# Two layers with attention, routed experts and coupling: the choice of tokens moved ahead, and the last output taken through diagonals of the gate

## The chip, the cores and the metric

The kernel runs on one core of a Trainium2 chip. The metric is the device time of one execution, in microseconds (us). Of before, three runs are given; the profile is of a fourth execution.

## The reference

The input x has 8 batches of 512 tokens with 256 channels, float32. Two layers follow one another; in each, `mod = silu(c) @ wmod` gives for every batch two shifts, two scales and two gates (the gates kept away from zero), and

```
h = layernorm(x) * (1 + ca) + sa;   x = x + ga * attention(h)
h = layernorm(x) * (1 + cb) + sb;   x = x + gb * ffn(h)
```

Layer 0: attention is causal softmax attention with 16 query heads of 16 channels, rotary embedding and one key and value head. Its ffn is a layer of 16 experts where each expert chooses tokens:

```
probs = softmax(h @ Wg + bg, over the tokens)
vals, idx = top_k(probs per expert, 64)          # per batch and expert
tok = h[idx]
out = (relu(relu(tok@w1+b1)@w2+b2)@w3+b3) * vals
outputs = zeros.at[idx].add(out)
```

Layer 1: attention is linear attention (elu + 1, causal running sums). Its ffn is three rounds of a coupling: a four layer network with gelu gives one gate per token, and

```
coupling = 0.1 + adaptive_range * (0.7*gf + 0.3*tf - 0.5) * 2
out = out + coupling * twist(out)                # twist swaps the channel halves, with signs
```

## The kernel before, in words

**Engines and their order.** The program order of all five engines' queues is written by hand: each engine carries out its instructions in the order in which the code issues them. Independent parts are Python generators ("lanes") that `Steps.run` advances in turn. A lane has a rank, which says who is served first, and a pace: `steps.rank(rank, every, phase)` lets it advance at every second (or `every`-th) step only. `steps.until("maxima", 7)` holds a lane until another has reported that event. A `yield` more or less in a lane therefore moves every instruction behind it relative to the other lanes.

**Layer 0, attention.** `batch(b)` is one lane per batch: `made_ready` (layer norm, projections, rotary embedding), `maxima` (the scores once, for the row maxima: PE L691/L701, DVE reductions L727 and L734, maxima L740, transposes L748, and L753, which puts the maxima into the queries), `heads_of` (the scores again, PE L793; ACT exponentials L815; POOL masks L820; PE values L775) and `finished` (PE transposes L845, DVE L850 and L852 which divide by the sums, L860, output projection L874, x += on DVE L880, a copy of x to memory, `xs`, L884, layer norm L563 to L572 with `bn_rstd` on POOL, gate logits L900, the modulation of the normalised tokens L914 on POOL, and the tokens to memory, `xg`, L916). At the end of `heads_of`, POOL adds the gated output bias to x (L830). Two batches overlap: heads of one beside maxima of the next. The modulation reads a row that a DMA brings (L891).

**Layer 0, experts.** `experts_side` (L940) waits for `ready` of batch 7 (the last), opens its buffers, waits for `maxima` of batch 7, and calls `choose(0)` for batches 0 to 3 (`choose(1)` is for batches 4 to 7). `choose` (L1002) holds 64 rows, an expert of a batch each, with 512 probabilities: softmax, then eight rounds of DVE's MAX8 (L1027), FIND_INDEX8 (L1028) and MATCH_REPLACE8 (L1031), two copies (`twice`, L1033/L1034), PE transposes (L1038), and small operations that make the indices `gidx` and `slot` and the values `valc`. `begin` gathers the tokens of three items and starts the weights of two. An item is one expert with the 128 tokens that two pairs of batches chose for it, twice (two indirect DMAs of 128 rows); there are 32 items, 16 for each half of the batches: experts 0 to 15 of the first half, then 8 to 15 and 0 to 7 of the second, so that eight weight sets are used again (`KEPT`). `run` (L1119) does per item: weights (`fetch_up_to`, on SP's queue, twice an item), gather of item i+3 (two indirect DMAs on POOL, L1103), ACT's scaling of item i-2 by its values (L1195), first layer (PE L1159, relu on DVE L1166), transposes of item i+1 (PE L1148, ACT L1152), scatter of item i-2 (two indirect DMAs on POOL that add into `xs`, L1202), last layer of item i-1 (PE L1179, DVE L1184), second layer of item i (PE L1159, relu on ACT L1168). In the middle (item 19) the first half of x is read back from `xs`. `choose(1)` is a generator that `run` advances twice an item; when a gather needs indices that are not made yet, the loop in `gather` drains the rest of it at once. Tokens have 4 buffers, `y` 3, `y0` 2.

**Layer 1.** Linear attention by batches (L1324 to L1568), its norm's `bn_rstd` on POOL (L1336 to L1340), `xh` on ACT (L1344), products (L1358, L1451, L1466). Then rounds of the coupling for pairs of batches n = 0 to 3 (`rounds`, L1795), where only PE's order is by hand. One round of a pair holds its state transposed, g (channels by tokens): `first_layer` (PE L1753; it also makes `still`, the part of the new g that does not depend on the gate), `later_layers` (L1805: w2 L1811, w3 L1821, w4 L1827, tanh on ACT L1831, m = (tanh + slope) x other half on DVE L1838, new g = still + or - m on DVE L1844). `finish` (L1851) multiplies g by the gate gb on ACT (`gated`, L1858), transposes it on PE (L1869), adds x on DVE into `res` (L1874, two buffers) and sends it out. The last pair's third round and its `finish` stand alone at the end of the program.

The change touches `heads_of`, `finished`, `experts_side`, `choose`, `open_first`, `begin`, `run` and `rounds`.

Of the kernel before, what the change touches and what calls it, by code (L numbers as in the profile page):

```python
# [13 lines left out]
F32 = mybir.dt.float32  # L14
# [8 lines left out]
P = 128  # L23
# [424 lines left out]
def layer0(net, steps):  # L448
# [311 lines left out]
    def heads_of(b, kT, qT):  # L760
# [66 lines left out]
        yield  # L827
        yield from values(3)
        for i in range(NT):
            nc.gpsimd.tensor_tensor(net.x[b][:, i, :], net.x[b][:, i, :], bg, ALU.add)  # L830
        yield
        return oT, wg

    def finished(b, oT, wg):
# [72 lines left out]
        for j in range(NT):  # L907
            nc.sync.dma_start(
                out=net.logits[b // NBP][b2 * NE : (b2 + 1) * NE, j * P : (j + 1) * P],
                in_=lg[32 * j : 32 * j + NE, :],  # L910
            )
        for row, how in zip(mod_rows, (ALU.mult, ALU.add)):
            for i in range(NT):
                nc.gpsimd.tensor_tensor(xh2[:, i, :], xh2[:, i, :], row, how)  # L914
            yield
# [24 lines left out]
    def experts_side():  # L940


        yield from steps.until("ready", B - 1)
        ready.close()
        experts.open_first()
        yield from steps.until("maxima", B - 1)
        yield from experts.choose(0)
        yield from experts.begin()
        yield from steps.until("heads", B - 1)
        early.close()  # L950
        experts.open()
        yield from experts.run(choices)
        experts.close()
        past.add(("experts",))
# [14 lines left out]
class Experts:  # L969
# [32 lines left out]
    def choose(self, half):  # L1002
# [31 lines left out]
        nc.vector.tensor_copy(twice[:, 1], vals.unsqueeze(1).to_broadcast([R, 2, TOPK]))  # L1034
        yield
        ps = net.mm()
# [30 lines left out]
        self.valc.append(valc)  # L1067
        yield

# [5 lines left out]
    def open_first(self):  # L1075

        self.tp = self.pool("t", 4)
        self.first_wp = self.pool("v", 2)

    def open(self):  # L1080
# [27 lines left out]
    def begin(self):  # L1108
        last = list(range(NE - self.KEPT, NE))
        self.items = [(0, e) for e in range(NE)] + [(1, e) for e in last]  # L1110
        self.items += [(1, e) for e in range(NE - self.KEPT)]
        self.tok, self.w = {}, {}
        for i in range(3):
            self.gather(i)
            if i < 2:
                self.w[i] = self.weights(i)
            yield

    def run(self, choices):  # L1119
# [15 lines left out]
        def gather(i):  # L1135
            if i < n_items:
                while len(self.gidx) <= items[i][0]:
                    next(choices)
                self.gather(i)
# [90 lines left out]
        for i in range(n_items + 2):  # L1230
            fetch_up_to(i + self.KEPT - 1)
            gather(i + 3)
            weighted(i - 2)
# [10 lines left out]
            if i == NE + 3:  # L1244
                read_back(0)
            fetch_up_to(i + self.KEPT - 1)
            self.steps.past.add(("item", i))
# [336 lines left out]
class Coupling:  # L1584
# [202 lines left out]
    def rest(self, out):  # L1787
        net, nc, tc = self.net, self.net.nc, self.net.tc
        with ExitStack() as ctx:
            self.ctx = ctx  # L1790
            gp = self.new_pool("f1g", 4, "right")
            pool = self.new_pool("f1", 2, "left")
            self.rounds(gp, pool, out)

    def rounds(self, gp, pool, out):  # L1795
# [9 lines left out]
        def later_layers(n, h1):  # L1805
# [43 lines left out]
            yield  # L1849

        def finish(n):  # L1851
            g, _ = self.state[n]
# [47 lines left out]
        with tc.manual_schedule(engines={nc.tensor.engine}):  # L1900
            done = (0, self.now)
            seen = {0: 1}
            between.append(prepare(2))
            for n in order[1:]:
                seen[n] = seen.get(n, 0) + 1
# [20 lines left out]
                done = (n, now)  # L1926
            later = later_layers(*done)
            for _ in range(3):
                take(later)
                fill(2)  # L1930
            fill(20)
            all_of(finish(done[0]))

# [78 lines left out]
```

## Time and profile before

| | |
|---|---|
| three runs | 1163.57, 1161.17, 1160.54 us, median 1161.17 |
| profiled execution | 1161.49 us; span of its instructions 1159.8; mean granted clock of TensorE 0.973 |
| busy: PE, DVE, ACT, POOL | 1084.9, 735.9, 573.3, 531.5 us (94, 63, 49, 46% of the span) |
| experts, 484 to 718 us: PE, DVE, ACT, POOL | 208.6, 81.8, 75.7, 178.2 busy of 234 |
| rounds of the coupling, 985 to 1145: the same | 159.8, 102.1, 85.7, 1.2 busy of 160 |
| last 15 us, 1145 to 1160: the same | 4.5, 8.3, 3.7, 0 busy; granted clock 0.58 |

Times in the profile are us from the span's start. A line of a timeline holds start, duration, engine, line of the code, operation, tiles (output <- inputs), how many instructions it groups, and in brackets the idle time before it and what ended it. A line of waits holds who waited for what, us in total, times, and the longest. A line of windows holds the stretch, its length, then busy time and instructions of PE, PEld, DVE, ACT and POOL, the granted clock, the DMA share and GB/s. Line numbers are those of before, unless it is said that they are of after; after's are higher by 1 to 6 in the attention and the experts (L830 is L831, L914 is L917, L1038 is L1045).

### The profile page before, as it was taken

The page shows a single profiled execution, that of the slowest core. Times are in us where ns is not written, and L with a number is a line of the kernel's source. Part 1 is how long each engine was busy: PE and PEld are TensorE (multiplying, and loading weights), DVE is VectorE, ACT ScalarE, POOL GpSimd, SP SyncE. Part 2 cuts the span into 40 slices and gives each one's busy share as a digit, 9 for nine tenths or more (in the row PEclk, how much of TensorE's full clock was granted, in tenths as well). Part 3 has the DMA queues.
Part 4 walks back from the last instruction along what each step waited for, and adds up shares of the span by engine and source line. Part 5 has one row for each costly group of instructions (what it writes and reads, how often), then busy time and mean ns, then how long its engine had stood idle before and what let it go on. Part 6 is the DMA issues. An engine that isn't in the chain of part 4 may idle for free. (4 is left out here: it accounts for less than half of the span.)

```text
span 1159.8 us, 20967 instructions
## 1 busy us (share of the span) xinstructions
PE 1084.9 (94%) x8282; PEld 675.1 (58%) x8282; DVE 735.9 (63%) x1444; ACT 573.3 (49%) x1061; POOL 531.5 (46%) x625
## 2 busy tenths in 40 slices
PE   4889999999999999889898989799999999999996
PEld 3545555555555555478676777466776666444433
DVE  3887777777777777622652322767768666766665
ACT  2255666666665657625232243544545543555544
POOL 4413344435353626568777787556545554000000
PEclk9889999999999999989899999899999999999997
DMA  6200010101101011387857944400000000000102
GB/s 208 90 1 1 1 28 25 29 26 29 42 12 50 5 50 44 91 272 208 204 89 186 241 83 61 114 6 6 6 2 6 7 6 2 0 1 19 54 1 73
DMA packets 67970, 69.02 MB, mean 60 GB/s; under 512 B 10216, under 2 KB 64544, under 8 KB 67872
## 3 DMA queue, kind: packets, MB, share of 16 engines
q1 hardware_dynamic: 55024, 49.32, 13.7%
q0 software_dynamic: 12288, 16.79, 8.4%
q8 instruction: 65, 1.06, 0.4%
q10 hardware_dynamic: 560, 1.58, 0.4%
q14 instruction: 33, 0.27, 0.1%
HBM read 46.38 MB, written 21.01 MB: 58 GB/s over the span
## 5 line engine op out<-in xcount | busy, mean ns | idle before, releaser
L815 ACT ACTIVATE e<-mm 128x512 f32<-128x512 f32 x320 | 171.6, 599 | 104.3 <-PE mm L793 90.7
L734 DVE TENSOR_REDUCE pm<-mm 128x4 f32<-128x512 f32 x256 | 162.2, 681 | 50.0 <-PE mm L701 49.0
L691 PE MATMUL mm<-kT,qT 32*128 32x128 f32 (+3 forms) x1024 | 192.3, 471 | 0.6 <-DVE pm L727 0.4
L793 PE MATMUL mm<-qT,kT 32*128 32x128 f32 (+3 forms) x1024 | 177.1, 465 | 0.0
L820 POOL TENSOR_SCALAR_AFFINE_SELECT e<-e 128x512 f32<-128x512 f32 x128 | 86.1, 693 | 186.7 <-ACT e L815 170.2
L1202 POOL DMA_INDIRECT xs<-y,slot x64 | 102.7, 1604 | 35.2 <-issue 11.3
L793 PEld LDWEIGHTS mm<-qT,kT 32*128 32x128 f32 x1024 | 81.5, 184 | 44.7 <-issue 21.0
L691 PEld LDWEIGHTS mm<-kT,qT 32*128 32x128 f32 x1024 | 92.7, 187 | 19.8 <-issue 4.7
L1753 PE MATMUL mm<-g,cn_w 128*128 128x512 f32 x192 | 93.2, 606 | 0.0
L775 PE MATMUL mm<-e,vaug 128*32 128x512 f32 (+3 forms) x1024 | 79.1, 437 | 2.2 <-POOL e L820 2.2
L1103 POOL DMA_INDIRECT tok<-xg,gidx x64 | 63.9, 998 | 19.4 <-issue 14.3
L1534 POOL TENSOR_SCALAR_AFFINE_SELECT am<-am 128x1024 f32<-128x1024 f32 x32 | 45.9, 1435 | 58.1 <-ACT am L1532 58.1
L1166 DVE TENSOR_SCALAR hid<-mm,eb 128x512 f32<-128x512 f32 x32 | 24.0, 750 | 73.0 <-PE mm L1159 73.0
L1168 ACT ACTIVATE hid<-mm,eb 128x512 f32<-128x512 f32 x32 | 22.0, 687 | 91.9 <-PE mm L1159 91.9
L1179 PE MATMUL mm<-ew,hid 128*128 128x256 f32 x256 | 63.9, 395 | 1.1 <-ACT hid L1168 1.1
L1184 DVE SCALAR_TENSOR_TENSOR y<-mm,eb,gb 128x512 f32<-128x512 f32 x32 | 24.0, 750 | 63.5 <-PE mm L1179 63.4
L1159 PE MATMUL mm<-hid,ew 128*128 128x256 f32 x256 | 62.2, 387 | 0.0
L1159 PE MATMUL mm<-tokT,ew 128*128 128x256 f32 x256 | 61.2, 382 | 0.1
L1358 PE MATMUL mm<-hT,w1qkv 128*128 128x512 f32 x128 | 60.9, 618 | 0.0
L1838 DVE SCALAR_TENSOR_TENSOR m<-th,slope,g 128x512 f32<-128x512 f32 x48 | 34.0, 748 | 40.4 <-ACT th L1831 40.4
L701 PEld LDWEIGHTS <-identb 128*128 128x128 bf16 x320 | 18.8, 98 | 64.4 <-issue 57.1
L1753 PEld LDWEIGHTS mm<-g,cn_w 128*128 128x128 f32 x192 | 33.1, 190 | 39.8 <-issue 37.1
(243 smaller groups left out, 2234.2 us busy)
## 6 DMA issues: line engine op xcount, KB each, us to landing
ew<-in_L_ffn_w SPq DMA_DIRECT2D x72, 256.0 KB, 6.8
x<-in_L_attn_x SPq DMA_DIRECT2D x8, 512.0 KB, 7.6
xs<-x SPq DMA_DIRECT2D x8, 512.0 KB, 3.0
xg<-xh SPq DMA_DIRECT2D x8, 512.0 KB, 3.3
x<-xs SPq DMA_DIRECT2D x8, 512.0 KB, 9.2
out<-res SPq DMA_DIRECT2D x16, 256.0 KB, 2.2
ga_row<-gate_a SPq DMA_DIRECT2D x16, 128.0 KB, 3.1
mod_row<-rows SPq DMA_DIRECT2D x16, 128.0 KB, 4.3
```

The lines of the kernel that those rows point to most:

```text
L691: nc.tensor.matmul(strips[j][:, at : at + nk], qT[g][rows_of(j), p, i * P : (i + 1) * P], kT[rows_of(j), p, :nk], start=(n == 0), stop=Fal ...
L734: nc.vector.tensor_reduce(pm[:, j, g, p, first : first + 4], strips[j].rearrange("q (a k) -> q a k", k=P), AX.X, ALU.max,)
L775: nc.tensor.matmul(av[32 * j : 32 * j + 32, c * P :], va[:, c, :], e[:, j, at : at + T - c * P], start=(a == 0), stop=(a == 3), skip_group ...
L793: nc.tensor.matmul(strips[j][:, at : at + T - c * P], kT[rows_of(j), p, c * P : (c + 1) * P], qT[g][rows_of(j), p, c * P :], start=(n == 0 ...
L815: nc.scalar.activation(e[:, j, :], strips[j], AF.Exp, scale=scale)
L820: nc.gpsimd.affine_select(out=own, in_=own, compare_op=ALU.is_ge, fill=0.0, base=0, pattern=[[0, 4], [1, P]], channel_multiplier=-1,)
L1103: self.net.nc.gpsimd.indirect_dma_start(out=tok[:, n, :], out_offset=None, in_=self.net.xg[half], in_offset=bass.IndirectOffsetOnAxis(ap=s ...
L1159: nc.tensor.matmul(ps[:, o * C : (o + 1) * C], w[i][n][:, k, o * P : (o + 1) * P], src[:, k, :], start=(k == 0), stop=(k == 1),)
L1179: nc.tensor.matmul(ps[:, n * C : (n + 1) * C], hid2[i][:, k, n * P : (n + 1) * P], w[i][2][:, k, :], start=(k == 0), stop=(k == 1),)
L1202: nc.gpsimd.indirect_dma_start(out=net.xs[2 * half + n], in_=y[i][:, n, :], in_offset=None, out_offset=bass.IndirectOffsetOnAxis(ap=self.s ...
L1358: nc.tensor.matmul(ps, w[:, k, n * P : (n + 1) * P], hT[:, k, :], start=(k == 0), stop=(k == 1))
L1753: nc.tensor.matmul(ps, self.w1[:, k, o * P : (o + 1) * P], g[k][bb], start=(k == 0), stop=(k == 1),)
```

## The change

1. The adds of the output bias for batch 7 (L830) and the modulation of batches 6 and 7 (L914) go from POOL to DVE.
2. `choose(0)` no longer waits for the maxima of batch 7: it begins two steps after batch 7 is ready, one step in three. Three yields instead of one stand ahead of `choose(1)`'s transposes, and both lose the last yield.
3. Tokens have 5 buffers, four items are gathered ahead instead of three, and the first two weight sets are started when the buffers are opened.
4. The second call of `fetch_up_to` in an item is made from item 6 on only.
5. For the last pair of batches, six POOL operations make diagonal matrices of the gate (`gate_diagonals`), issued at the start of the rounds. In its last round (`last_layers`) PE multiplies `still` and m by these diagonals and accumulates both in one bank (16 products for each, with the token side as the stationary matrix); that is g times the gate, transposed. DVE adds x to it into four buffers of their own. The new g, `gated` and the transposes of `finish` fall away for this pair.

The diff, with the copied w2, w3 and w4 layers of `last_layers` cut:

```diff
--- before.py
+++ after.py
@@ -826,8 +826,9 @@
         wg, bg = net.gated_by(pool, wo, bo, ga)
         yield
         yield from values(3)
+        engine = nc.vector if b == B - 1 else nc.gpsimd
         for i in range(NT):
-            nc.gpsimd.tensor_tensor(net.x[b][:, i, :], net.x[b][:, i, :], bg, ALU.add)
+            engine.tensor_tensor(net.x[b][:, i, :], net.x[b][:, i, :], bg, ALU.add)
         yield
         return oT, wg
 
@@ -909,9 +910,11 @@
                 out=net.logits[b // NBP][b2 * NE : (b2 + 1) * NE, j * P : (j + 1) * P],
                 in_=lg[32 * j : 32 * j + NE, :],
             )
+        engine = nc.vector if b >= B - 2 else nc.gpsimd
         for row, how in zip(mod_rows, (ALU.mult, ALU.add)):
             for i in range(NT):
-                nc.gpsimd.tensor_tensor(xh2[:, i, :], xh2[:, i, :], row, how)
+                engine.tensor_tensor(xh2[:, i, :], xh2[:, i, :], row, how)
             yield
         nc.sync.dma_start(
             out=net.xg[b // NBP][b2 * T : (b2 + 1) * T, :].rearrange("(i p) c -> p i c", p=P),
@@ -943,8 +946,11 @@
         yield from steps.until("ready", B - 1)
         ready.close()
         experts.open_first()
-        yield from steps.until("maxima", B - 1)
+        steps.rank(4, 3)
+        yield
+        yield
         yield from experts.choose(0)
+        steps.rank(4)
         yield from experts.begin()
         yield from steps.until("heads", B - 1)
         early.close()
@@ -1032,7 +1038,8 @@
         twice = pool.tile([R, 2, 2, TOPK], F32, name="twice")
         nc.vector.tensor_copy(twice[:, 0], idx.unsqueeze(1).to_broadcast([R, 2, TOPK]))
         nc.vector.tensor_copy(twice[:, 1], vals.unsqueeze(1).to_broadcast([R, 2, TOPK]))
-        yield
+        for _ in range(1 + 2 * half):
+            yield
         ps = net.mm()
         for a in range(2):
             nc.tensor.transpose(
@@ -1065,7 +1072,6 @@
         self.slot.append(slot)
         self.gidx.append(gidx)
         self.valc.append(valc)
-        yield
 
     def pool(self, name, bufs):
         return self.stack.enter_context(
@@ -1074,8 +1080,9 @@
 
     def open_first(self):
 
-        self.tp = self.pool("t", 4)
+        self.tp = self.pool("t", 5)
         self.first_wp = self.pool("v", 2)
+        self.w = {i: self.weights(i) for i in range(2)}
 
     def open(self):
         self.hp, self.yp = self.pool("h", 2), self.pool("y", 3)
@@ -1109,11 +1116,9 @@
         last = list(range(NE - self.KEPT, NE))
         self.items = [(0, e) for e in range(NE)] + [(1, e) for e in last]
         self.items += [(1, e) for e in range(NE - self.KEPT)]
-        self.tok, self.w = {}, {}
-        for i in range(3):
+        self.tok = {}
+        for i in range(4):
             self.gather(i)
-            if i < 2:
-                self.w[i] = self.weights(i)
             yield
 
     def run(self, choices):
@@ -1135,7 +1140,7 @@
         def gather(i):
             if i < n_items:
                 while len(self.gidx) <= items[i][0]:
-                    next(choices)
+                    next(choices, None)
                 self.gather(i)
 
         def turn(i):
@@ -1229,7 +1234,7 @@
         yield
         for i in range(n_items + 2):
             fetch_up_to(i + self.KEPT - 1)
-            gather(i + 3)
+            gather(i + 4)
             weighted(i - 2)
             if i < n_items:
                 hid[i] = layer(i, 0, tokT[i], "hid")
@@ -1243,7 +1248,8 @@
                 hid2[i] = layer(i, 1, hid[i], "hid2")
             if i == NE + 3:
                 read_back(0)
-            fetch_up_to(i + self.KEPT - 1)
+            if i >= 6:
+                fetch_up_to(i + self.KEPT - 1)
             self.steps.past.add(("item", i))
             next(choices, None)
             yield
@@ -1790,6 +1796,7 @@
             self.ctx = ctx
             gp = self.new_pool("f1g", 4, "right")
             pool = self.new_pool("f1", 2, "left")
+            self.last = self.new_pool("f1l", 1, "left")
             self.rounds(gp, pool, out)
 
     def rounds(self, gp, pool, out):
@@ -1846,6 +1853,91 @@
                         ALU.add if h == 0 else ALU.subtract,
                     )
             self.state[n] = (new, offs)
+            yield
+        def gate_diagonals(n):
+            sides = {}
+            for bb in range(2):
+                b = 2 * n + bb
+                for h in range(2):
+                    kept = self.last.tile([P, P], F32, name=f"kept{h}{bb}")
+                    nc.gpsimd.tensor_scalar(
+                        kept, net.ident, net.modT[1][:, GB, h, b : b + 1], 1.0, ALU.mult, ALU.mult
+                    )
+                    moved = kept
+                    if h:
+                        moved = self.last.tile([P, P], F32, name=f"moved{bb}")
+                        nc.gpsimd.tensor_scalar(moved, kept, -1.0, 1.0, ALU.mult, ALU.mult)
+                    sides[bb, h] = kept, moved
+            return sides
+        def last_layers(n, h1, sides):
+            g, _ = self.state[n]
...
+            ms = {}
+            for bb in range(2):
+                th = pool.tile([P, T], F32, name=f"th{bb}")
+                nc.scalar.activation(th, ps[bb], AF.Tanh, bias=self.b4, scale=0.5)
+                for h in range(2):
+                    ms[bb, h] = pool.tile([P, T], F32, name=f"m{h}{bb}")
+                    nc.vector.scalar_tensor_tensor(
+                        ms[bb, h], th, self.slope, g[1 - h][bb], ALU.mult, ALU.mult
+                    )
+            banks = {}
+            for part in range(2):
+                for bb in range(2):
+                    b = 2 * n + bb
+                    for ip in range(NT // 2):
+                        if part == 0:
+                            banks[bb, ip] = net.mm()
+                        ps = banks[bb, ip]
+                        for ii in range(2):
+                            i = 2 * ip + ii
+                            for h in range(2):
+                                src = ms[bb, h] if part else h1["still"][h][bb]
+                                nc.tensor.matmul(
+                                    ps[:, ii * C + h * P : ii * C + (h + 1) * P],
+                                    src[:, i * P : (i + 1) * P], sides[bb, h][part],
+                                    start=(part == 0 and ii == 0 and h == 0), stop=(part == 1),
+                                    skip_group_check=True,
+                                )
+                        if part == 0:
+                            continue
+                        res = self.last.tile([P, 2, C], F32, name="last", bufs=4)
+                        nc.vector.tensor_tensor(
+                            res, net.x[b][:, 2 * ip : 2 * ip + 2, :],
+                            ps.rearrange("p (i c) -> p i c", i=2), ALU.add,
+                        )
+                        at = ip * 2 * P
+                        nc.sync.dma_start(
+                            out=out[b, at : at + 2 * P, :].rearrange("(i p) c -> p i c", p=P),
+                            in_=res,
+                        )
             yield
 
         def finish(n):
@@ -1901,6 +1993,7 @@
             done = (0, self.now)
             seen = {0: 1}
             between.append(prepare(2))
+            sides = gate_diagonals(NBP - 1)
             for n in order[1:]:
                 seen[n] = seen.get(n, 0) + 1
                 while self.state.get(n, (None, None))[1] is None:
@@ -1924,12 +2017,12 @@
                 if seen[done[0]] == CYCLES:
                     between.insert(0, finish(done[0]))
                 done = (n, now)
-            later = later_layers(*done)
-            for _ in range(3):
-                take(later)
-                fill(2)
+            later = last_layers(*done, sides)
+            take(later)
+            fill(2)
+            take(later)
             fill(20)
-            all_of(finish(done[0]))
+            take(later)
 
 
 @with_exitstack
```

## The prediction

> **What bounds the kernel now.** I read the busy shares and the 40 slices first, then the stretches between stages, then the waits of the expert stage (484 to 734 us), then single instructions of POOL, PE and DVE. PE is busy 94% of the span; it is nearly full everywhere but in three places, and the change touches each. First, the expert stage. Its waits in this stretch (columns: waiter, what it waited for, sum us, times, longest):
>
> ```profile
> PE mm L1148 <- DMA tok<-xg,gidx: 24.0, 23, 5.0
> POOL tok L1103 <- issue: 14.3, 48, 0.5
> POOL xs L1202 <- DMA xs<-y,slot: 9.0, 8, 2.8
> ```
>
> PE waits for gathered tokens. Behind that stands POOL, whose steady item has no gap but some 0.30 an instruction (start, duration, line, idle before):
>
> ```profile
> 584.78 1.63 POOL L1202 DMA_INDIRECT xs<-y,slot  x1 [0.30 <-ACT hid L1168]
> 586.71 1.58 POOL L1202 DMA_INDIRECT xs<-y,slot  x1 [0.30 <-issue]
> 588.59 1.01 POOL L1103 DMA_INDIRECT tok<-xg,gidx  x1 [0.30 <-PE mm L1179]
> 589.91 0.99 POOL L1103 DMA_INDIRECT tok<-xg,gidx  x1 [0.31 <-issue]
> ```
>
> So an item costs POOL 3.81 for its scatters and 2.61 for its gathers, 6.42 together (first layers of items 10 to 30 stand 6.71 apart). PE needs three layers of 1.73 and .43 of transposes, 5.62 (items 2 to 4: 511.50, 517.12, 522.74). POOL sets the pace, and it also begins late:
>
> ```profile
> 484.74 1.25 POOL L1103 DMA_INDIRECT tok<-xg,gidx  x1 [0.19 <-issue]
> 486.30 0.95 POOL L1103 DMA_INDIRECT tok<-xg,gidx  x1 [0.30 <-issue]
> 487.27 2.77 POOL L914 TENSOR_TENSOR xh<-xh,mod_row 128x256 f32<-128x256 f32 x4
> 490.01 2.77 POOL L830 TENSOR_TENSOR x<-x,bo_g 128x256 f32<-128x256 f32 x4
> 492.94 0.99 POOL L1103 DMA_INDIRECT tok<-xg,gidx  x1 [0.16 <-issue]
> ```
>
> Item 1's gather waits behind 5.5 us of attention arithmetic; item 1 starts at 501.72, 11.5 after item 0. Second, DVE in the attention before (busy after the five names' times; third pair is DVE):
>
> ```profile
> 415.00:420.00 5.00, 5.00 (x59) 2.04 (x55) 1.68 (x3) 2.38 (x6) 0.64 (x1) 1.00 0.00 0
> 435.00:440.00 5.00, 5.00 (x44) 1.97 (x48) 4.68 (x8) 3.63 (x9) 2.84 (x7) 1.00 0.00 0
> 440.00:445.00 5.00, 5.00 (x72) 3.28 (x68) 2.08 (x4) 4.55 (x10) 0.64 (x1) 1.00 0.00 0
> ```
>
> The choice of tokens goes into these gaps now. Third, the tail: w4's last matmuls end at 1144.77, the span at 1159.8.
>
> ```profile
> 1149.01 2.37 PE L1869 MATMUL mm<-ident,gated 128*128 128x128 f32 x8 [4.24 <-ACT gated L1858]
> 1154.17 1.44 DVE L1874 TENSOR_TENSOR res<-x,mm 128x512 f32<-128x512 f32 x2 [1.71 <-DMA out<-res]
> ```
>
> **The change part by part.** The sum is made against the profiled execution, 1161.49 us (span 1159.8 and 1.7 around it), .3 above the median 1161.17.
>
> *A. Early choice, maxima of batch 7 (412 to 456).* In before, the choice takes DVE from 452.99 to 481.4. Now maxima and two sums (.83), probabilities and the rest of the first round (2.35) and six rounds at .69+.68+.67 and gaps, 2.16 (13), about 16 us, stand ahead of the last L753. DVE's gaps in 412 to 447 add to 11.9. Bounds: 16 late if no gap is used, 4.1 if all are. I laid its instructions into the gaps one by one, each reduction behind the choice ops that precede it: the queue runs .65, 1.8, 3.7 and then about 6 late; L753's last pairs start 6.5 late (454.8, not 448.24). Scores of batch 7 (PE L793, 450.60) wait for them: 5.7 to 6.4; I take 6.4.
>
> *B. Heads of batch 7 (450 to 486).* What leaves: PE's wait of 1.47 for `twice` (L1038). What comes: 8 gathers on POOL (1.25 and .30 at first) among masks L820. Each is a quarter or a half of the mask gaps there (3 to 4.7 us idle), so only those that meet a ready mask cost: some 3 us at the second values, less the 1.47 and slow matmuls, net +1.4. Bounds: -1.7 (none met) and +10 (8 x 1.25, all met). Then transposes of tokens (L1148) no longer wait: -1.7 (.42, .34 and the masks' .89). First expert matmul: 490.23 + 6.4 + 1.4 - 1.7 = 496.3.
>
> *C. First items.* Four gathers are done when they begin and the fifth has a buffer. Item 1 at +5.5, item 2 at +12.9 (batch 7's attention output is interleaved), then 5.62 each. First scatter 496.3 + 13.2 = 509.5 (511.34 before); the second stands behind batch 7's `bn_rstd`, whose statistics stand behind the relu of item 3 on DVE: 522 (522.66). One set of weights an item until the seventh is costed at nothing: two sets are there ahead, and each lands in 6.8 us, below two items of 5.62; without that cover one item waits up to 6.8.
>
> *D. Steady items.* From second scatter to end of scatter 29 (717.70): before 195.0 us = 29 scatter pairs x 3.81 (110.5) + 25 gather pairs x 2.61 (65.3) + L914 of batch 7 (3.37 + 2.78 = 6.15) + `bn` work 2.85 + 10 idle. After: 110.5 + 24 x 2.61 (62.6) + 2.85 = 176, and idle: 2.4 of the trailing scatters, 3.7 at the read-back, some 2 elsewhere, 8. End at 522 + 184 = 706, 11.7 earlier; if the 10 stays idle, 9.4 earlier. I take 11. What follows (`bn_rstd` of the next layer, `xh`, projections) moves along. The 8 adds and 8 multiplies of L914 and 4 of L830 that go to DVE take .42 each by L314 (481.92, POOL idle), 8.4 us, beside PE's work (DVE busy 82 of 234 here); L314 beside POOL's L914 took .85 (446.42). So 8.4 to 17.
>
> The Trainium skill (SBUF — State Buffer, "SBUF: two separate sides") says that a DVE instruction with two SBUF inputs and a GpSimd instruction reading SBUF lock one another out for a whole instruction. The pair .42 and .85 agrees; no row has such an add beside an indirect DMA. By it each of the 20 adds might wait 1.25, a gather: a rival, below.
>
> *E. Second choice.* Its last rounds come at once at item 12, since that gathers item 16: three rounds (6.5) and two copies on DVE; PE's transposes (L1038 in the numbers of before) stand ahead of item 12's layers: PE stops some 6, and matmuls after such a stop are slow:
>
> ```profile
> 559.37 1.13 PE L1148 MATMUL mm<-ident,tok 128*128 128x128 f32 x4 [5.00 <-DMA tok<-xg,gidx]
> 560.29 3.57 PE L1179 MATMUL mm<-ew,hid 128*128 128x256 f32 x8
> 563.70 1.89 PE L1159 MATMUL mm<-hid,ew 128*128 128x256 f32 x8
> ```
>
> 3.57 for 1.89 adds 1.7: PE 7.7 late. POOL gets its indices at 576.4 by this and would arrive there at 573 to 577, so it stops 0 to 3 us; four gathers lie ahead of PE's need. Costed within D's idle (the 2 us elsewhere).
>
> *F. End.* Leave: 4 adds to g (2 x 1.29), 4 `gated` on ACT (2 x 1.33), PE's wait of 4.24, DVE's of 1.71 on an outgoing buffer. Come: 32 fp32 products of 128x128 with diagonals in place of 16 transposes. At full speed one is .287 (L1547: six instructions .86, two to a product), at the halved clock of 1150 to 1160 up to .6. `still` products 1144.8 to 1149.4, `m` products behind m (1150.0) to 1154.0, last add 1154.7 against 1155.6: gain 1; the span ends 4.2 after the last add, as before (1155.6, 1159.8). Bounds: 3 gained (full clock) to 2 lost (halved for all 32). Six 128x128 POOL operations (by 128x512 ones of .94, 2 us at most) near 981 are costed at nothing: POOL is idle from 993; without that, 2.
>
> Sum: -11 -1 = -12: 1149.5 on the profile's scale, about 1149 for the median.
>
> **Rivals.**
> 1. *More.* All 11.9 of DVE's gaps are used (A +4.1), no gather meets a mask (B -1.7): items begin 4 to 7 us sooner than forecast, the second scatter 4, and waits for landings (9.0) shrink by 4: 1149 - 8 = 1141. For: the gaps exist. Against: one choice op of .7 in front of a reduction shifts its successors.
> 2. *Slower.* DVE's 16 us all delay L753, and POOL's gathers all delay masks (10): first matmul +24 (16 + 10 - 1.7) instead of +6, second scatter 540 instead of 522, all after it 18 later than forecast: 1149 + 18 = 1167. It decides from a start 18 us late (first matmul 508), where the saving of 12 is eaten. For: DVE was busy 87, 77 and 94% in the 5 us from 410, 425 and 435. Against: the 5 us stretches above, of 1.68 and 2.08 busy.
> 3. *Little.* POOL's work falls, but its scatters wait for landings (pitch 4.4 in the last three items, three `y` buffers) or PE at 5.62 with the stop of E (7.7) sets the pace: 3 to 5 gained, 1157.
> 4. *The lock.* 20 adds on DVE wait for gathers: up to 20 x 1.25 = 25 us of DVE, of which batch 7's adds lie ahead of its output: first items and its statistics 4 later, 1153.
>
> **How the numbers follow.** Forecast .56, more .14, little .14, lock .08, slower .08. Predicted 1149; range 1139 to 1159 takes in A's and B's ends short of the slower case and leaves that out. This kernel's time can be told from no change at about 0.3%, 3.5 us: faster .85 (all but the slower case and half of little, which lies near the bound), same .07, slower .08.
>
> **What would show it.** Right: last L753 of batch 7 near 455; first expert matmul near 496; first two scatters near 509 and 522; POOL at 6.4 an item; a stop of PE near 6 ahead of the second choice's transposes at item 12; first matmul of the layer 1 attention near 722 (733.1); last addition 5 us before the end. Wrong: first expert matmul past 506, an item above 6.6, DVE adds above 1 us each behind gathers, or a tail longer than 15 us behind w4.

## The result, and the profile after

The changed kernel took 1155.81 us (median of 7 runs, 1152.97 to 1160.02) against 1160.79 for the one before (7 runs): ratio 0.9955, interval 0.9934 to 0.9976, a gain of 5.0 us by the medians and 5.2 by the ratio. Two more measurements, below, gave 0.9945 and 0.9953. Forecast was a gain of 12. The first profile of the changed kernel is of its slowest run, 1160.02 (span 1158.3); two more are of 1152.5 and 1154.4.

The waits of the expert stage (484 to 734 us; waiter, what it waited for, sum, times, longest), first profile of after:

```profile
ACT y L1200 <- DMA xs<-y,slot: 28.6, 6, 7.3
POOL xs L1207 <- ACT y L1200: 16.7, 12, 7.5
POOL xs L1207 <- DMA xs<-y,slot: 12.1, 8, 2.7
PE mm L1045 <- DVE twice L1040: 6.6, 1, 6.6
```

PE's wait for gathered tokens (24.0 before) has gone from the list. In its place scatters wait longer for the scatters before them to land (12.1 for 9.0), partly by way of ACT, which must not overwrite `y` while it is being sent (28.6 for 6.1). The single instructions, POOL's timeline:

```profile
554.87 1.62 POOL L1207 DMA_INDIRECT xs<-y,slot  x1 [2.70 <-DMA xs<-y,slot]
...
562.50 1.61 POOL L1207 DMA_INDIRECT xs<-y,slot  x1 [1.54 <-DMA xs<-y,slot]
...
571.00 1.61 POOL L1207 DMA_INDIRECT xs<-y,slot  x1 [2.42 <-DMA xs<-y,slot]
...
640.14 1.63 POOL L1207 DMA_INDIRECT xs<-y,slot  x1 [4.15 <-ACT y L1200]
```

The early choice stops PE once, and its clock is halved behind the stop, for a part of the next 10 us (PE's timeline; then the windows, where 0.69 and 0.63 are the mean granted clock):

```profile
434.41 0.70 PE L793 MATMUL mm<-qT,kT 32*128 32x256 f32 x4
436.84 1.39 PE L691 MATMUL mm<-kT,qT 32*128 32x256 f32 x3 [1.72 <-DVE pm L734]
```
```profile
435.00:440.00 5.00, 3.28 (x20) 1.89 (x18) 3.67 (x8) 1.08 (x2) 2.15 (x6) 0.69 0.00 0
440.00:445.00 5.00, 5.00 (x29) 1.54 (x32) 4.93 (x10) 2.86 (x6) 1.08 (x2) 0.63 0.00 0
```

And the tail on DVE: four adds one behind the other, none waiting for an outgoing buffer (first and last):

```profile
1151.47 0.69 DVE L1932 TENSOR_TENSOR last<-x,mm 128x512 f32<-128x512 f32 x1 [0.61 <-PE mm L1923]
...
1154.15 0.69 DVE L1932 TENSOR_TENSOR last<-x,mm 128x512 f32<-128x512 f32 x1 [0.21 <-PE mm L1923]
```

Places of the same events in before and in the three profiles of after (us):

| | before | forecast | first | second | third |
|---|---|---|---|---|---|
| scores of batch 7 (L793) | 450.6 | 456.3 to 457.0 | 456.0 | 454.4 | 456.0 |
| first expert matmul | 490.2 | 496.3 | 499.0 | 496.8 | 499.0 |
| second scatter | 522.7 | 522 | 525.2 | 522.9 | 525.2 |
| scatter 29 ends | 717.7 | 706 | 716.5 | 712.8 | 714.5 |
| between these two | 195.0 | 184 | 191.4 | 189.9 | 189.4 |
| layer 1's L1466 | 733.1 | 722 | 731.9 | 727.6 | 729.9 |
| w4's end to span's end | 15.0 | 14 | 11.5 | 11.5 | 11.6 |
| span | 1159.8 | 1147.8 | 1158.3 | 1150.8 | 1152.7 |

### The profile page after: what moved, and what is told of

Same layout as the page of the kernel before. It is cut to its first block, busy times and chain, and to the rows that moved or that the text cites. A ratio compares the mean times of both kernels' runs of the same rounds, so it can differ in the third digit from the quotient of the medians.

```text
span 1158.3 us, 21048 instructions
## 1 busy us (share of the span) xinstructions
PE 1092.6 (94%) x8330; PEld 683.9 (59%) x8330; DVE 739.3 (64%) x1460; ACT 570.8 (49%) x1057; POOL 519.3 (45%) x611
## 3 DMA queue, kind: packets, MB, share of 16 engines
q8 instruction: 66, 1.08, 0.4%
## 4 chain that ended last, share of the span: by engine, by line
PE 79%; DVE 9%; POOL 5%; issue 3%; ACT 2%; DMA 1%; ACTq 0%; DVEq 0%; POOLq 0%
PE mm L793 11%; PE mm L1759 8%; PE mm L1164 7%; PE mm L691 6%; PE mm L775 5%; PE mm L1364 4%; PE mm L701 4%; PE mm L1184 4%; PE mm L1818 3%; PE mm L1526 3%; PE mm L596 3%; PE mm L1560 2%; PE mm L875 2%; PE mm L1381 2%; PE mm L279 2%
## 5 line engine op out<-in xcount | busy, mean ns | idle before, releaser
L691 PE MATMUL mm<-kT,qT 32*128 32x128 f32 (+3 forms) x1024 | 195.1, 476 | 2.3 <-DVE pm L734 1.7
L793 PE MATMUL mm<-qT,kT 32*128 32x128 f32 (+3 forms) x1024 | 179.9, 473 | 0.8 <-DVE o_tok L853 0.8
L793 PEld LDWEIGHTS mm<-qT,kT 32*128 32x128 f32 x1024 | 82.2, 187 | 46.8 <-issue 23.9
L1164 PE MATMUL mm<-tokT,ew 128*128 128x256 f32 x256 | 64.0, 395 | 4.8 <-ACT y L1200 2.6
L1164 PEld LDWEIGHTS mm<-tokT,ew 128*128 128x128 f32 x256 | 49.5, 197 | 13.3 <-ACT tokT L1157 3.2
L1845 DVE SCALAR_TENSOR_TENSOR m<-th,slope,g 128x512 f32<-128x512 f32 x44 | 31.0, 747 | 39.8 <-ACT th L1838 39.8
```

The source lines that it names most:

```text
L691: nc.tensor.matmul(strips[j][:, at : at + nk], qT[g][rows_of(j), p, i * P : (i + 1) * P], kT[rows_of(j), p, :nk], start=(n == 0), stop=Fal ...
L793: nc.tensor.matmul(strips[j][:, at : at + T - c * P], kT[rows_of(j), p, c * P : (c + 1) * P], qT[g][rows_of(j), p, c * P :], start=(n == 0 ...
L1164: nc.tensor.matmul(ps[:, o * C : (o + 1) * C], w[i][n][:, k, o * P : (o + 1) * P], src[:, k, :], start=(k == 0), stop=(k == 1),)
```

## The experiments

e1 to e4 ran on one chip, e5 to e8 on a second, e9 to e12 and f1 to f4 on a third, g1 and g2 on a fourth. Ratios are to before on the same chip, with intervals; times of runs on different chips are compared by their ratios. Each run has one profile.

**e1, the changed kernel again.** 

> The changed kernel unaltered, for a second profile. In the first one PE's clock was halved in two stretches where before shows none, 435 to 445 us and 872 to 882 us (granted clock .63 to .69 and .5), 3.2 to 3.4 us lost in each. Theory (these two are chance of one execution, and the change itself is worth some 5 to 8 us): one or both stretches are missing in this profile and its span is 3 to 7 us below 1158.3. Rival (they belong to the change: DVE's choice stops PE at 435 each time): the stretch at 435 is there again and the span is within 1 us of 1158.

Measured: 1154.36, 0.9945 (0.9931 to 0.9959). Half of each: the stop of 1.72 at 435 is there again, in every profile with the choice at every third step, with 1.7 to 3.6 us lost to the clock behind it (1.7 in this one, by its granted clock of 0.88 and 0.78 from 435 to 445); the stretch at 872 is missing. The span is 7.5 us below the first profile's.

**e2, one set an item; e3, read-back spread; e4, four `y`.** The diffs in this order:

```diff
-            if i >= 6:
-                fetch_up_to(i + self.KEPT - 1)
...
-            if i == NE + 3:
-                read_back(0)
+            if NE + 3 <= i < NE + 3 + NBP:
+                read_back(0, (i - NE - 3,))
...
-        self.hp, self.yp = self.pool("h", 2), self.pool("y", 3)
+        self.hp, self.yp = self.pool("h", 2), self.pool("y", 4)
```

> The changed kernel with one set of weights an item throughout: the second fetch of an item is gone also from item 6 on. Theory (the saved POOL work is given back as waits for scatters to land, since the DMA engines are full at 548 to 570 us with weights: shares of 1.09 to 1.14, POOL idle 5.8 us in three waits at 554.87, 562.50 and 571.00): these waits shrink below 2 us and the time falls by 3 to 5 us against the changed kernel. Rival (the end of the expert stage is set by something later, the read-back at 640 us or the trailing scatters, or by the late start): the waits go and the time is the same within 1 us.

> The changed kernel with the first half's x read back one batch an item (items 19 to 22) instead of four at item 19. Theory (same cause, DMA engines full at 630 to 650 us, POOL idle 4.15 and 1.58 us ahead of scatters): the two waits shrink by 3 to 4 us and so does the time. Rival (waiting is only moved to later items): within 1 us of the changed kernel.

> The changed kernel with four buffers for y instead of three. If late landings hold POOL by way of the buffers (ACT's scaling waits 28.6 us for scatters to land in the profile of after), one more item of slack, 6.4 us, takes most of the idle time and 3 to 6 us of the time. If they hold it directly (a scatter adds to the same memory as the one before and has to wait for its landing), nothing changes within 1 us.

Measured: 1157.10, 0.9967 (0.9954 to 0.9981); 1154.22, 0.9936 (0.9923 to 0.9948); 1154.51, 0.9944 (0.9928 to 0.9961). The waits stayed: 2.62, 1.63 and 1.57 in e2; 3.39 and 2.09 in e3; 2.62, 1.64, 1.68 and 3.76 in e4. None of the three gained what its theory has: e3 and e4 took the time of e1, and e2 lay 2.7 above it (the intervals overlap a little). Buffers for `y` are not what holds POOL; a scatter is held by the landing of the one before it. In e2 15 weight transfers still left at one go (545.7 to 560 us), since SP had stood at batch 7's logits until 540.

**e5, batch 7's logits from ACT's queue.**

```diff
-            nc.sync.dma_start(
+            (nc.scalar if b == B - 1 else nc.sync).dma_start(
                 out=net.logits[b // NBP]...
```

> The changed kernel with the four copies of batch 7's gate logits started from ACT's queue instead of SP's. In the second profile of the changed kernel SP stands from 526 to 538 us at these copies (they wait for ACT's logits), 18 weight transfers queue behind them and then fill the DMA engines from 544 to 566 us (shares 1.02 to 1.13), with and without the second fetch. Theory (that flood, not the pace of two sets, makes the scatters land late): weights flow from 526 on, POOL's three waits at 552, 560 and 568 us (2.46, 1.71, 1.58) shrink by 3 to 5 us in sum, and the time falls by 2 to 5 us against the changed kernel. Rival (weights wait for their buffers anyway, or the layer 1 weights alone fill the engines): waits stay, same time within 1 us.

Measured: 1154.39, 0.9930 (0.9918 to 0.9942), the time of e1. Six transfers left sooner (18 instead of 12 from 518 us on), but 12 more queued behind batch 7's tokens at 543.7, and the waits were 1.49, 2.49 and 2.25: moved, not removed.

**e7, the arithmetic back on POOL** (both `engine` lines to `nc.gpsimd`). 

> The changed kernel with the modulation of batches 6 and 7 and the bias of batch 7 on POOL as before. Theory (POOL sets the pace from the second scatter on, and batch 7's modulation is 6.1 us of its time there; the 8.3 us of batch 6's modulation and batch 7's bias lie ahead of the second scatter among gathers that are ahead): 5 to 9 us slower than the changed kernel, which is the greater part of the whole gain. Rival (the pace is set by landings, and a later gather costs nothing): within 2 us of the changed kernel.

Measured: 1158.36, 0.9962 (0.9947 to 0.9977), 4.0 above e5 on the same chip, between theory and rival. Second scatter to scatter 29 took 194.3, 2.9 to 4.9 more than in after, for 6.15 of work: a part of it takes the place of waiting (190.6 in e5).

**e8, the choice every fourth step** (`steps.rank(4, 4)`). 

> The changed kernel with the early choice taking every fourth step instead of every third, so that fewer of its rounds stand ahead of the reductions of batch 7's scores. Theory (PE's stop at 435 us and the slow clock behind it come from a round of the choice in front of a reduction): the stop goes or is below 1 us, no clock below .9 between 430 and 450, first expert matmul 3 to 5 us earlier than 497 to 499, time 2 to 5 us less. Rival (the later indices delay the gathers, or the rounds stop PE in another place): first matmul no earlier, time within 1.5 us.

Measured: 1152.75, 0.9915 (0.9895 to 0.9935), 1.6 below e5, less than the theory's 2 to 5, and the intervals overlap. As the theory has it, there is no stop and no slow clock at 435, and the first matmul comes at 490.9, sooner still than expected; but its gathers begin at 485.3, no earlier than with the late choice (485.8 in e6).

**e9, weights of eight experts only.**

```diff
-            if half == 0 or e not in last:
+            if half == 0 and e < self.KEPT:
                 w[i] = self.weights(e)
             else:
-                w[i] = w[items.index((0, e))]
+                w[i] = w[e % self.KEPT]
```

> The changed kernel with weights of experts 0 to 7 only: the other experts compute with these, so 24 MB of weights shrink to 6 and the output is another; every instruction of the engines is still issued, only the weight transfers from item 8 on are left out. Theory (POOL's waits for scatters at 552 to 568 us, 5.8 us in the second profile, and at 636 and 644, 5.4 us, come from DMA engines filled by weights; spacing the same transfers otherwise could not take them away): both groups shrink to 2 us or less each and the time falls by 5 to 9 us against the changed kernel. Rival (a scatter waits for the scatter before it whatever else runs, or the second choice and the read-back alone do it): the waits are within 1.5 us of what they were and so is the time.

Measured: 1150.88, 0.9912 (0.9886 to 0.9937), 4 to 5 us below the changed kernel by ratio, across chips; that is less than the 5 to 9 expected. (The weight transfers fell from 72 to 24 of 256 KB, 18 MB to 6; the 24 MB of the text above is a slip.) POOL's scatters in e9, then windows (DMA share is the next to last column, POOL the fifth pair), first of after, then two of e9:

```profile
555.12 1.62 POOL L1207 DMA_INDIRECT xs<-y,slot  x1 [3.72 <-DMA xs<-y,slot]
...
561.53 1.61 POOL L1207 DMA_INDIRECT xs<-y,slot  x1 [0.31 <-ACT hid L1173]
...
567.92 1.61 POOL L1207 DMA_INDIRECT xs<-y,slot  x1 [0.30 <-DMA xs<-y,slot]
```
```profile
560.00:565.00 5.00, 5.00 (x27) 4.41 (x26) 4.86 (x11) 1.79 (x4) 3.15 (x3) 1.00 1.12 333
```
```profile
550.00:555.00 5.00, 5.00 (x27) 4.40 (x26) 2.24 (x4) 1.47 (x4) 1.09 (x2) 1.00 1.00 234
560.00:565.00 5.00, 5.00 (x27) 4.41 (x26) 4.86 (x12) 2.13 (x4) 4.15 (x3) 1.00 0.49 92
```

From 560 to 565 after had a share of 1.12, e9 has 0.49. Where the engines are free, the waits are gone (0.30 is POOL's own gap); where they still fill at 545 to 555 (batch 7's tokens and layer 1's weights; a wait of 3.72) and at the read-back (3.26 left of 4.15), they stay. Second scatter to scatter 29 fell to 186.1.

**e10, the new end alone** (before, with the last pair's new end and nothing else of the change). 

> The kernel before with only the new end: diagonals of the gate in the last round, the adds into four buffers. Theory (from the end of w4 to the end of the span 11.5 us in four profiles of the changed kernel against 15.0 before, clock kept full by the products): 3 to 4 us below the kernel before. Rival (the six POOL operations and the fuller banks ahead of the rounds give part of it back): 0 to 2 us below.

Measured: 1157.67, 0.9973 (0.9959 to 0.9986): 3.1 us, the theory; w4's end to span's end 11.5.

**e11, the moved arithmetic alone.** 

> The kernel before with only the POOL work of batches 6 and 7 moved to DVE. Theory (POOL's arithmetic stands ahead of gathers at 487 to 498 us and among the items at 540 to 549, 14.6 us in sum, and 418 ns an add on DVE cost nothing): gather of item 1 at 488 instead of 492.9, last scatter 6 to 9 us earlier, time 6 to 9 us below the kernel before. Rival (only the 6.1 us behind the second scatter count, and some of them turn into waits for landings): 2 to 5 us.

Measured: 1157.79, 0.9968 (0.9955 to 0.9982), 3.7 us: the rival. Scatter 29 ends at 712.9 (717.7), but the first items are no earlier: item 1 at 504.1 for 501.7, with engines at a standstill as in g2 (below). From the second scatter to scatter 29 it took 188.6, where e10 on the same chip took 195.7: the 6.15 of arithmetic came out whole there, in a profile of e11's fastest run. e10 and e11 gain 6.8 in sum and the whole change 5.2 to 6.4 (on other chips): what is left of it, the early choice, the items ahead and the pace of the weights, is not shown to gain anything.

**e12, early choice, gathers behind the heads** (`begin` after `experts.open()`). 

> The changed kernel with the early choice kept, but with its first gathers behind the heads of batch 7, not among the masks. It tells the two costs of the early choice apart. If DVE's order is the main one (scores of batch 7 at 454.4 and 456.0 instead of 450.6, slow clock at 435): first expert matmul at 495 to 498, time within 2 us of the changed kernel. If the gathers among masks are (PE's wait of 4.66 at 486): first expert matmul 3 to 5 us earlier than 496.8 to 499 and the time 3 to 5 us less.

Measured: 1158.37, 0.9978 (0.9966 to 0.9989), neither branch: first matmul at 502.7, since PE now waits for its tokens (first gather 491.7). By ratio it is some 3 us behind the changed kernel, on another chip and with a short standstill (2.3) of its own: so it is only likely that the gathers among the masks are worth more than the 3 us that they cost.

**e6, f4 and g2, the late choice, with g1, the changed kernel beside it.**

```diff
-        steps.rank(4, 3)
-        yield
-        yield
+        yield from steps.until("maxima", B - 1)
         yield from experts.choose(0)
-        steps.rank(4)
```

> The changed kernel with the choice where it was before: after the maxima of batch 7. All else of the change stays. Theory (the early choice costs more than it gives: PE stops 1.7 us at 435 with a halved clock for 6.8 us, L753 comes 6.5 us later, and gathers stand among masks, while the late choice held PE 1.47 us only): first expert matmul at 489 to 492 instead of 497 to 499, no slow clock at 435, last scatters 3 to 8 us earlier, time 3 to 8 us below the changed kernel. Rival (the gathers must be ready when the heads end): PE waits for tokens at items 0 to 3 for 6 us or more, time 2 to 6 us above the changed kernel.

> The late choice once more, for its time beside the three others and a second profile. If its gain is of the order of work and not chance: 1145 to 1149 us, first expert matmul at 490 to 492, no slow clock between 430 and 450.

> The changed kernel, side by side with the late choice on one chip. 1153 to 1157 is expected on every chip, since its first weights come after the first items have begun (DMA share .2 at 495 to 500 us) and nothing stands still there.

> The late choice beside it. It took 1147 on one chip and 1159 on another; in the second profile ACT, DVE and POOL stand still for 7.9, 3.6 and 2.8 us between 491 and 503 us, released by what the profile calls remote, while the DMA engines are full (share .97 to 1.09); such waits are in seven of the eight profiles of that chip and in no other. If these stops make the difference, then in this pair the late choice is 6 to 9 us faster than the changed kernel where its profile has no such stops, and 0 to 5 us slower where it has them. If the early choice costs 8 us by itself, the late choice is faster either way.

Measured: e6 1147.01, 0.9871 (0.9854 to 0.9888); f4 1158.82, 0.9982 (0.9969 to 0.9995); g1 1155.84, 0.9953 (0.9939 to 0.9967); g2 1158.63, 0.9974 (0.9964 to 0.9985). After e6 the early choice seemed to cost 8 us; the pair g1 and g2 says the opposite for that chip, 2 to 3 us gained (the intervals overlap a little), as g2's text has it for a profile with stops. f4 missed its 1145 to 1149. What differs between e6 and g2 is a standstill. ACT's timeline, e6 and then g2 (the same code):

```profile
491.32 0.59 ACT L865 COPY oTd<-mm 128x512 f32<-128x512 f32 x1
493.85 0.59 ACT L1154 COPY tokT<-mm 128x512 f32<-128x512 f32 x1 [1.94 <-PE mm L1150]
```
```profile
499.61 0.59 ACT L865 COPY oTd<-mm 128x512 f32<-128x512 f32 x1 [7.11 <-issue]
502.54 0.59 ACT L1154 COPY tokT<-mm 128x512 f32<-128x512 f32 x1 [2.35 <-remote]
```

The profile shows nothing that this `oTd` waited for ("issue"), and PE had finished its input by 490.5. DVE and POOL start again at 502.49 and 502.78 ("remote" 4.99 and 2.58), item 1 at 507.2 instead of 496.3. In both runs the DMA engines are full there (0.79 to 1.08 in g2, 0.87 to 1.08 in e6), for with the late choice 12 weight transfers leave at 491, as the first items begin; in after they leave around 500 and the share at 495 to 500 is 0.20 to 0.51, and no such stop is seen. But e8's engines are as full (0.94 to 1.08 from 490 on) and nothing stands still there, so full engines alone do not make the stop. What the waiting engines lacked is not named by any view, and the cause stays open. Waits on "remote" between 484 and 512 us are in seven of the eight profiles of the third chip, in g2 on the fourth, and in no other.

**f1, f2, f3, variants of the late choice**: three items ahead, four token buffers; read-back in every third item; weights of eight experts as in e9. 

> The changed kernel with the late choice, and three items gathered ahead with four token buffers as before. Theory (with POOL free of arithmetic the four first gathers run in one piece, 485.8 to 496, and what is worth some 8 us beside the new end and the moved arithmetic is that PE no longer waits for items 1 to 3): within 2 us of the late choice (1147), since three in one piece are as good as four. Rival (the fourth gather ahead is what covers late landings): 3 to 8 us above it.

> The late choice with the first half's x read back one batch in every third item (19, 22, 25, 28) instead of four at once. Theory (the read-back fills the DMA engines for some 6 us and POOL waits 3.75 and 1.67 us behind it at 631 and 639): with two items between the pieces both waits fall below 1.5 us, time 2 to 4 us below the late choice. Rival (each piece costs its own late landing): no change within 1 us.

> The late choice with weights of experts 0 to 7 only (the other experts compute with these; the output is another; only weight transfers are left out). Theory (landings behind weights are a fixed 4 to 5 us of the expert stage, in whichever way it begins): 3 to 5 us below the late choice, as it was 3.5 to 5 below the changed kernel. Rival (with the earlier start the stage is bound by POOL alone): within 1.5 us of the late choice.

Measured: 1157.35, 0.9968 (0.9956 to 0.9981); 1156.48, 0.9957 (0.9942 to 0.9973); 1152.56, 0.9919 (0.9904 to 0.9935), beside f4's 0.9982. All four have the standstill. Against f4, f1 is no worse, so the fourth item ahead is not shown to be worth anything. f2 has waits of 2.99 and 1.14 at the read-back for f4's 4.02 and 1.46, and is 2.3 us faster, with intervals that overlap a little: the time is as expected, the waits are not. f3 is 6.3 faster, more than expected, and the rival (bound by POOL alone) is out.

No version is shown to beat the changed kernel on more than one chip; the late choice was faster on one (1147.0 against e5, which stands in for the changed kernel there, with 1154.4) and slower on another.

## Why the prediction was wrong

The direction held and so did most steps; the size was 5 for 12.

- **D is the step that failed:** "After: 110.5 + 24 x 2.61 (62.6) + 2.85 = 176, and idle: 2.4 of the trailing scatters, 3.7 at the read-back, some 2 elsewhere, 8." The work came out at 176. The idle time was 13.4 to 15.4: three waits at 552 to 571 (4.8 to 5.8 net of POOL's own gap of .30), read-back 4.8 to 5.1 for 3.7, trailing scatters about 3.5 for 2.4, one of 1.1 to 1.4 at 531. So 3.6 to 5.6 of the forecast 11 were gained. Other runs tell which of D's three savings failed, by the stretch from second scatter to scatter 29 and POOL's idle time in it (what exceeds .30 in every gap above .45; it comes out 1 to 2 us above the idle time of the sums):

| | stretch | idle |
|---|---|---|
| before; e10 | 195.0; 195.7 | 11.9; 12.6 |
| e11, arithmetic moved, three items ahead | 188.6 | 11.1 |
| f1, late choice, three items ahead | 190.1 | 12.3 |
| f4, the same with four ahead | 190.8 | 15.4 |
| after, three profiles | 191.4; 189.9; 189.4 | 16.5; 15.0; 14.5 |
| e9; f3, weights of eight experts | 186.1; 184.6 | 11.2; 9.4 |

The arithmetic's 6.15 can come out whole (e11). The pair of gathers (2.61) that leaves the stretch with a fourth item ahead came back as waiting: f1 to f4, PE's wait for tokens fell (10.5 to 2.4 between 515 and 716), POOL's idle time rose by 3.1 and the stretch got no shorter. And the idle time that was to shrink by 2 rose. I took before's waits for landings for a rest; where POOL asked for transfers sooner, on engines that weights, tokens and the read-back had already filled, it waited for them to land. e9 and f3 show that the weights are part of the cause; e2 and e5 that pace and queue are not the way to mend it. How much of the rise belongs to each part of the change is open: these are single profiles. This is the rival "little" in its mechanism (landings). I had read before's waits, but not its DMA shares, which stood at .71 over the whole stage and at .99 to 1.13 from 500 to 530.
- **A was right in sum** (scores of batch 7 3.8 to 5.4 later, for 5.7 to 6.4, of which 6.4 was taken), but it has no stop of PE (1.72, and a halved clock that lost 1.7 to 3.6), and no waits for `o_tok` behind those scores (.74 and .83). DVE's gaps from 412 to 447 add to 10.6 (35 less 24.4 busy), not 11.9.
- **B was too small:** 3.2, not 1.4. From batch 7's first scores to its gate logits PE took 39.5 us for 34.7; 1.6 of that are the waits for `o_tok`. Second profile, PE waiting for masks that stand behind gathers on POOL, the last two at 483.3 and 484.7:

```profile
486.42 0.97 PE L775 MATMUL mm<-e,vaug 128*32 128x256 f32 x8 [4.66 <-POOL e L820]
```

- **C was right** within 2 us on the first scatter (509.1 to 511.4, forecast 509.5); the second came 1 to 3 late.
- **E was right:** 6.63 of standstill, the next eight matmuls 3.78, and no wait of POOL for indices.
- **F was mis-sized:** 3.1 to 3.5 gained, its bound for a full clock, not 1. The `still` products fill the wait for tanh (32 instructions 3.84), the granted clock is 1.00 from 1145 to 1155 (0.74 and 0.50 in before), and the `m` products follow at .22 each.
- **The lock** costs a little, and by masks, not gathers. Batch 6's and 7's modulation took 1.42 or 1.43 for four adds throughout, beside gathers too; only L831 took longer, beside two masks that themselves took 1.50 for 1.23 (in e6 two masks took 2.78 beside eight such adds):

```profile
492.07 1.43 DVE L917 TENSOR_TENSOR xh<-xh,mod_row 128x256 f32<-128x256 f32 x4 [13.52 <-PE mm L279]
493.42 2.29 DVE L831 TENSOR_TENSOR x<-x,bo_g 128x256 f32<-128x256 f32 x4
498.53 1.42 DVE L917 TENSOR_TENSOR xh<-xh,mod_row 128x256 f32<-128x256 f32 x4
```

The Trainium skill (SBUF — State Buffer, "SBUF: two separate sides") has the lock against GpSimd instructions that read SBUF; a mask does, and these rows agree. My rival applied it to gathers, and no row here shows that. The .85 that the prediction set beside POOL's L914 (446.42 to 447.27) ran beside masks, too: they end at 447.00, and L914 begins at 446.96.

The rival "slower" has its mechanism in the trace (A and B), at 6.5 to 8.8 us instead of 24. In sum for the second profile: 5.6 late at L1466, 2.5 early in the tail, some 3 above the forecast of 1149.5: 1152.5. That it lies no further off is in part luck: F's surplus covers a part of what D, A and B lost.

## What to carry to other kernels

Letting an engine issue its transfers sooner gains only as much as the transfers land sooner: read the DMA share in the stretch before pricing it, and expect saved time as waits for landings where it stands near 1 (a fourth item ahead gave nothing, f1 and f4). Measure the parts of a change alone as well: arithmetic taken from that engine came out whole by itself (e11), in part beside the other changes (e7). Work put into an engine's gaps is paid where one instruction of it stands ahead of a result that PE needs; a gap's sum does not show that. Time rivals side by side on one chip: one kernel here changed by 12 us between chips while the kernel before stayed within 1.3.

## What was not expected of the hardware

One and the same wait of PE, 2.40 us, is followed by a halved clock in one execution and not in another. PE in before and in the first profile of after, then windows behind the wait, one of before and three of after (the clock is third from the end):

```profile
875.32 0.71 PE L1520 MATMUL mm<-qz,k1T 32*128 32x256 f32 x8 [2.40 <-POOL qz L1501]
```
```profile
874.38 1.24 PE L1526 MATMUL mm<-qz,k1T 32*128 32x256 f32 x8 [2.39 <-POOL qz L1507]
```
```profile
876.00:878.00 2.00, 2.00 (x12) 0.76 (x11) 1.95 (x4) 1.09 (x3) 0.72 (x1) 1.00 0.03 8
```
```profile
876.00:878.00 2.00, 2.00 (x3) 0.72 (x3) 2.00 (x4) 0.79 (x2) 1.13 (x1) 0.50 0.00 0
878.00:880.00 2.00, 2.00 (x10) 0.67 (x12) 0.94 (x2) 0.63 (x2) 0.48 (x1) 0.50 0.00 0
880.00:882.00 2.00, 2.00 (x21) 1.47 (x14) 0.92 (x2) 1.47 (x4) 0.00 (x0) 0.85 0.00 0
```

In after the granted clock is .5 until 880, and 3.2 us are lost (L1466 to w4's end: 414.9; 411.7 in before, 411.7 in the second profile). All 20 profiles have this wait, and the slow clock followed it in 7 of them, whatever the change; so it can make a part of the spread of 7 us between runs. The Trainium skill (TensorE: Matmul & The Clock Gate, Part 1) tells of a free-running window of about 3.4 us, with the moment of a transition depending on where in it the work falls. That would fit the chance; no run here tests it. It warns of gaps above some 3.4 us; here 1.72 and 2.40 were enough, and the measurement decides.
